# Two input channels become one work item over pairs of PSUM banks in the filter stage of a convolution kernel, and two small outputs change their PSUM pool

## The chip, the cores and the metric

The kernel runs on one core of a Trainium2 chip. The metric is the device time of one execution in microseconds (us). The profile and the trace come from one execution taken by the hardware profiler. Engines: PE is the matrix engine (PEld its weight loads), DVE the vector engine, ACT the scalar engine, POOL the GpSimd engine, SP the queue that issues most of the DMAs. PSUM has eight banks of 2 KB a partition, each of which holds 128x512 fp32 values[...].

## The reference

Two layers on an input of (4, 512, 512, 16). The change concerns the filter of the first layer only:

```python
# layer 0: x = x + conv(groupnorm(x)), with a filter given as a ratio of polynomials
a = jnp.pad(denumerator, ((0, 0), (0, 0), (1, 0), (1, 0)), constant_values=1.0)
b = jnp.pad(numerators, ((0, 0), (0, 0), (0, 0), (1, 0), (1, 0)), constant_values=0.0)
H_truncated = jnp.fft.rfft2(b, s=(l1, l2)) / jnp.fft.rfft2(a, s=(l1, l2))   # 512 x 512, 16 x 16 channels
h_truncated = jnp.fft.irfft2(H_truncated, s=(l1, l2))
H = jnp.fft.rfft2(h_truncated, s=(2 * l1, 2 * l2))
H_full = h0 + H[0]
X = jnp.fft.rfft2(x, s=(2 * l1, 2 * l2), axes=(-3, -2))
y = jnp.fft.irfft2(jnp.einsum('...hwi,ijhw->...hwj', X, H_full), ...)[..., :l1, :l2, :]
# layer 1: x = x + a 3x3 convolution of groupnorm(x) with norms, arccos and tanh
```

Numerator and denominator are polynomials of 9 x 9 terms for each of 16 x 16 pairs of channels (i in, j out).

## The kernel before

The kernel is a chain of stages. `filter_phase`, the first, computes the filter and writes it to `g_d` in DRAM; the transform of the input, the product with the filter, the way back and the second layer follow and are not touched. During the filter stage a generator, `beside`, also computes statistics of the input: one BATCH_NORM_STATS2 on DVE in every second step of the loop.

**Items.** A work item is (j, kp, h, i): output channel j, half kp of the frequencies k1 (two chunks k of 128, on the partitions), half h of the frequencies k2 (128, on the free axis), input channel i. There are 16 x 2 x 2 x 16 = 1024 items, and the loop takes two neighbouring i at a time, so 512 pairs, 32 for each j. One pass of the loop is called a step, p.

**A pair passes through three steps** (`new`, `mid`, `last`), so that a step works on three pairs:

- new: `polynomials` (L349): for each of the two channels two PSUM tiles of one bank each, pa (denominator) and pb (numerator), shape [128, k, c, 128] with c real or imaginary; sixteen recorded matmuls. `evict` on ACT: copy of pa to SBUF as `a` (L357), the squares of its real part to `sq` (L359) and of its imaginary part in place (L360).
- mid: `products` on DVE: m = pb·a (L366), x = pb·a with c swapped (L368), dn = the two squares added (L370). `terms` on POOL (L374, L375): numerator times conjugate denominator. Later in the step DVE's reciprocal of dn (L504), and `quotient` on POOL, sp = m/|a|² (L379).
- last: `edge` on ACT for h = 0: column k2 = 0 of sp is replaced from z (L384). `taps` (L395): 32 recorded matmuls of sp with a constant, into two PSUM tiles `pg`. `placed` on ACT: four copies of pg into the stage `st` (L406), which goes to `g_d` when i has run through.

**Beside it runs `odd(j - 1)`**: it reads back g_d of the output channel before (`ev_in`, L433), multiplies by a constant (`pt`, L447), copies (`ot`, L452) and writes to g_d (L453). `next(rest)` stands twice in a step, and each time copies the pt before and issues the next (four recorded matmuls of 128x512). For the first j there is nothing of it yet. After the loop the last `odd` runs alone.

**Rare parts.** `quad` runs in steps with p % 16 = 0, 2, 4 and 14: eight small matmuls into the PSUM tile `pu` (L332) and an ACT copy to `u` (L335), the polynomials over k1 of four channels, used two steps later. `weights(j + 1)` spreads over some ten steps of each j; once in it, four matmuls go into the tile `pz` (L285), and ACT copies it to `zs` (L293).

**PSUM.** Three pools share the eight banks: `ps_ab` with four buffers (pa and pb of two channels), `ps_g` with two (`pg`), `ps_t` with two, tag `t`, shared by pt, pu and pz:

```python
pt = ps_t.tile([P, 32 * C], F32, name="pt", tag="t")
pu = ps_t.tile([P, 2, N // 2], F32, name="pu", tag="t")
```

**Order.** `InOrder` keeps PE, DVE, ACT and POOL in the order in which the program issues. SP is ordered by a scheduler. In a step the order on PE is: pt (first `next(rest)`), the taps of `last`, the polynomials of `new`, pt (second `next(rest)`), and then pu or pz if it is their turn. On ACT: copy of the pt before, `edge`, `placed`, copy of the pt before, `evict`, then u or zs.

Of the kernel before, what the change touches and what calls it, by code (L numbers as in the profile page):

```python
# [40 lines left out]
F32 = mybir.dt.float32  # L41
# [3 lines left out]
PSUM = bass.MemoryType.PSUM  # L45

P = 128
N = 512
B = 4
C = 16  # L50
# [151 lines left out]
def bc(ap, axis, shape):  # L202
    return ap.unsqueeze(axis).to_broadcast(shape)
# [24 lines left out]
def filter_phase(tc, cst, h0, num, den, g_d, beside):  # L228
    nc = tc.nc
    with ExitStack() as ctx:  # L230
# [3 lines left out]
        ew = ctx.enter_context(tc.tile_pool(name="f_ew", bufs=2))  # L234
        stp = ctx.enter_context(tc.tile_pool(name="f_stage", bufs=4))
        evp = ctx.enter_context(tc.tile_pool(name="f_even", bufs=2))
        odp = ctx.enter_context(tc.tile_pool(name="f_odd", bufs=2))
        ps_ab = ctx.enter_context(tc.tile_pool(name="f_psab", bufs=4, space=PSUM))
        ps_g = ctx.enter_context(tc.tile_pool(name="f_psg", bufs=2, space=PSUM))
        ps_t = ctx.enter_context(tc.tile_pool(name="f_pst", bufs=2, space=PSUM))  # L240

        e1 = load_const(nc, cp, cst, "e1")
        e2 = load_const(nc, cp, cst, "e2").rearrange("p (s h n) -> p s h n", s=2, h=2)
# [5 lines left out]
        polys = {}  # L249

        def weights(j):
# [19 lines left out]
            v = sm.tile([18, 2, 4, C], F32, name="v")  # L271
            ev = sm.tile([18, 2, 2, C], F32, name="ev")
            od = sm.tile([18, 2, 2, C], F32, name="od")
            for n, t in enumerate((sa, sb)):
                for c in range(2):
                    q = 9 * c
# [3 lines left out]
            nc.vector.tensor_add(v[:, :, 0::2, :], ev, od)  # L280
            nc.vector.tensor_sub(v[:, :, 1::2, :], ev, od)
            yield
            pz = ps_t.tile([P, 4, 2, 4, C], F32, name="pz", tag="t")
            for k in range(4):
                nc.tensor.matmul(  # L285
                    pz[:, k].rearrange("p c v i -> p (c v i)"),
# [2 lines left out]
                    start=True,  # L289
                    stop=True,  # L290
# [29 lines left out]
            z = wt.tile([P, 4, 2, C], F32, name="z")  # L320
# [4 lines left out]

        def quad(j, kp, iq):

            pu = ps_t.tile([P, 2, N // 2], F32, name="pu", tag="t")
            for n in range(2):
                for i in range(4):  # L330
                    at = 32 * (i ^ 2 * n)
                    nc.tensor.matmul(pu[at : at + 32, n], polys[j][n][:, 4 * iq + i],  # L332
                                     e1[:, kp * (N // 2) : (kp + 1) * (N // 2)], start=True, stop=True)
            u = wt.tile([P, 2, N // 2], F32, name="u", bufs=6)
            nc.scalar.copy(u, pu)  # L335
            us[j, kp, iq] = u

        def polynomials(pair):

            for w in pair:
                w["pp"] = [ps_ab.tile([P, 2, 2, P], F32, name=f"pab{n}", tag="ab") for n in range(2)]
            for k in range(2):
                for w in pair:
                    for n in range(2):
                        at = 32 * (w["i"] % 4 ^ 2 * n)
                        q = slice(at, at + 18)
                        nc.tensor.matmul(  # L349
                            w["pp"][n][:, k].rearrange("p c n -> p (c n)"),  # L350
                            w["u"][q, n, k * P : k * P + P], e2[q, n, w["h"], :], start=True, stop=True,
                        )

        def evict(w):
            pa, _ = w["pp"]
            w["a"] = ew.tile([P, 2, 2, P], F32, name="a", bufs=4)
            nc.scalar.copy(w["a"], pa)  # L357
            w["sq"] = ew.tile([P, 2, P], F32, name="sq", bufs=4)
            nc.scalar.activation(w["sq"], pa[:, :, 0], AF.Square)  # L359
            nc.scalar.activation(pa[:, :, 1], pa[:, :, 1], AF.Square)  # L360

        def products(w):

            (pa, pb), a = w.pop("pp"), w["a"]
            w["m"] = ew.tile([P, 2, 2, P], F32, name="m", bufs=4)
            nc.vector.tensor_mul(w["m"], pb, a)  # L366
            w["x"] = ew.tile([P, 2, 2, P], F32, name="x", bufs=2)
            nc.vector.tensor_mul(w["x"], pb, a[:, :, ::-1])  # L368
            w["dn"] = ew.tile([P, 2, P], F32, name="dn", bufs=3)
            nc.vector.tensor_add(w["dn"], w["sq"], pa[:, :, 1])  # L370

        def terms(w):
            m, x = w["m"], w["x"]
            nc.gpsimd.tensor_add(m[:, :, 0], m[:, :, 0], m[:, :, 1])  # L374
            nc.gpsimd.tensor_sub(m[:, :, 1], x[:, :, 1], x[:, :, 0])  # L375

        def quotient(w):
            w["sp"] = ew.tile([P, 2, 2, P], F32, name="sp", bufs=4)
            nc.gpsimd.tensor_mul(w["sp"], w["m"], bc(w["dn"], 2, [P, 2, 2, P]))  # L379

        def edge(w):
            if w["h"] == 0:
                kp = w["kp"]
                nc.scalar.copy(w["sp"][:, :, :, 0], w["z"][:, 2 * kp : 2 * kp + 2, :, w["i"]])  # L384

        def taps(pair):

            kp, i, h, j = (pair[0][k] for k in ("kp", "i", "h", "j"))
            pg = [ps_g.tile([P, 2, 2, 4, 32], F32, name=f"pg{u}", tag="pg") for u in range(2)]
            for n, w in enumerate(pair):  # L390
                for k in range(2):
                    for c in range(2):
                        for u in range(2):
                            q = slice(64 * u, 64 * u + 64)
                            nc.tensor.matmul(  # L395
                                pg[u][:, n, k].rearrange("p a x -> p (a x)"), w["sp"][q, k, c, :],
                                dinv[q, 2 * kp + k, c, :], start=(c == 0), stop=(c == 1),
                            )
            return pg

        def placed(pair, st, pg):

            kp, i, h, j = (pair[0][k] for k in ("kp", "i", "h", "j"))
            for u in range(2):
                for a in range(2):
                    nc.scalar.copy(  # L406
                        st[a].rearrange("p (q k u x) i -> p u k q x i", q=2, k=2, u=2)[:, u, :, :, :, i : i + 2],
                        pg[u][:, :, :, 2 * a : 2 * a + 2].rearrange("p n k q x -> p k q x n"),
                    )
            if i == C - 2:  # L410
                for a in range(2):
                    for q in range(2):
                        nc.sync.dma_start(
                            out=dram(g_d[h], None, a * G_ROW // 2 + ((32 * q + 16 * kp) * C + j) * 8 * C,
                                     [C * 8 * C, 16], [1, 8 * C]),
                            in_=st[a].rearrange("p (q r e) i -> p q r (e i)", q=2, e=8)[:, q],
                        )
# [41 lines left out]
        def odds():  # L459

            for j in range(C):
# [2 lines left out]
                yield from odd(j)  # L464

        work = [dict(j=j, h=h, i=i, kp=kp)
                for j in range(C) for kp in range(2) for h in range(2) for i in range(C)]
        done, us = [0], {}
        order = InOrder(tc, nc.tensor, nc.vector, nc.scalar, nc.gpsimd)
        rest = odds()  # L470
# [1 line left out]
            pass  # L472
        quad(0, 0, 0)
        coming = iter(())
        n_pairs = len(work) // 2
        for p in range(n_pairs + 2):
            new, mid, last = (work[2 * (p - k) : 2 * (p - k) + 2] if 0 <= p - k < n_pairs else [] for k in range(3))
            with order:
                next(rest)
            if last:  # L480
                if last[0]["i"] == 0:
                    st = [stp.tile([P, N // 2, C], F32, name=f"st{a}", tag="st") for a in range(2)]
                with order:
                    for w in last:
                        edge(w)
                    placed(last, st, taps(last))
                done[0] += 2
                for w in last:
                    w.clear()
            with order:  # L490
                for w in mid:
                    products(w)
                    terms(w)
            if new:
                for w in new:
                    w["u"], w["z"] = us[w["j"], w["kp"], w["i"] // 4], polys[w["j"]][2]
                with order:
                    polynomials(new)
            with order:
                next(rest)  # L500
                for w in new:
                    evict(w)
                for w in mid:
                    nc.vector.reciprocal(w["dn"], w["dn"])  # L504
                    quotient(w)
                j, kp, r = p // 32, p // 16 % 2, p % 16
                if r in (0, 2, 4) and p < n_pairs:
                    quad(j, kp, r // 2 + 1)
                elif r == 14 and p + 2 < n_pairs:
                    quad(j + kp, 1 - kp, 0)  # L510
                if p % 32 == 4 and j + 1 < C:
                    coming = weights(j + 1)
                next(coming, None)
                if p % 2:
                    next(beside, None)
# [914 lines left out]
```

## Time and profile before

| | |
|---|---|
| median of 3 runs | 16929.8 us (16927.85 to 16944.9) |
| the profiled execution | 16971.28 us, its span 16969.5 us |
| filter loop in the trace, first polynomial matmul to last taps | 23 to 3760 us |
| mean granted PE clock | 0.969; 1.00 from 600 to 3400 us |
| busy in the stretch 600 to 1000 us (400 us) | PE 387.96, DVE 367.14, POOL 301.47, ACT 261.40, PEld 225.64 us |
| DMA share and rate there | 0.83, 241 GB/s |

The program's stages have different limits, so that the shares of the whole span say little about the filter stage; a window inside of it says more. A matmul that the page calls busy is a pipelined one: its record is longer than the time after which the next can follow. Times from one start to the next are therefore used below where an engine's pace matters.

From the second j on the steps repeat. Measured from the first taps matmul of a step to that of the next, the 32 steps of j = 3, at 736.23 to 969.62 us, take 8.67 us eight times (the steps with a quad; one of them 8.87), 8.72 us once (the step with pz), 6.79 us ten times and 6.69 us thirteen times. The ten are steps at whose start `edge` stands (h = 0), the thirteen such without it.

### The profile page before, as it was taken

The page shows a single profiled execution, that of the slowest core. Times are in us where ns is not written, and L with a number is a line of the kernel's source. Part 1 is how long each engine was busy: PE and PEld are TensorE (multiplying, and loading weights), DVE is VectorE, ACT ScalarE, POOL GpSimd, SP SyncE. Part 2 cuts the span into 40 slices and gives each one's busy share as a digit, 9 for nine tenths or more (in the row PEclk, how much of TensorE's full clock was granted, in tenths as well). Part 3 has the DMA queues.
Part 4 walks back from the last instruction along what each step waited for, and adds up shares of the span by engine and source line. Part 5 has one row for each costly group of instructions (what it writes and reads, how often), then busy time and mean ns, then how long its engine had stood idle before and what let it go on. Part 6 is the DMA issues. An engine that isn't in the chain of part 4 may idle for free. (4 is left out here: it accounts for less than half of the span.)

```text
span 16969.5 us, 546571 instructions
## 1 busy us (share of the span) xinstructions
PE 15334.3 (90%) x233100; PEld 11354.6 (67%) x233100; DVE 10569.6 (62%) x22267; ACT 9051.1 (53%) x18799; POOL 10185.7 (60%) x10637
## 2 busy tenths in 40 slices
PE   7999999999998888889888888888888888988888
PEld 5555555554447777777777777777777777877777
DVE  8999999973335555555555555555555553347877
ACT  5666666652225555555555555555555552017888
POOL 7777777761116666666666666666666661137766
PEclk7999999999999999999999999999999999989999
DMA  4888888887658888888888888888888886885531
GB/s 135 235 236 238 232 233 242 232 237 222 187 179 320 321 323 324 320 322 320 317 325 324 323 323 323 320 318 323 320 325 323 320 311 246 295 293 174 166 112 69
DMA packets 2914701, 4543.45 MB, mean 268 GB/s; under 512 B 126114, under 2 KB 2094460, under 8 KB 2801422
## 3 DMA queue, kind: packets, MB, share of 16 engines
q1 hardware_dynamic: 2703070, 3836.37, 66.5%
q0 software_dynamic: 172336, 605.00, 9.3%
q10 hardware_dynamic: 36864, 67.13, 1.1%
q8 instruction: 1837, 30.10, 0.7%
q14 instruction: 594, 4.87, 0.1%
HBM read 3030.71 MB, written 1477.31 MB: 266 GB/s over the span
## 5 line engine op out<-in xcount | busy, mean ns | idle before, releaser
L822 PE MATMUL pg<-c_dg,g 64*128 64x128 f32 x32832 | 2834.4, 291 | 329.7 <-ACT gh L722 163.9
L838 PE MATMUL pm<-xe,gh 128*32 128x64 f32 x131328 | 2405.5, 222 | 571.9 <-issue 342.4
L838 PEld LDWEIGHTS pm<-xe,gh 128*32 128x32 f32 x131328 | 2015.6, 110 | 1175.5 <-issue 1001.6
L822 PEld LDWEIGHTS pg<-c_dg,g 64*128 64x128 f32 x32832 | 2281.4, 190 | 667.6 <-issue 264.5
L867 DVE TENSOR_TENSOR z<-zq,pz 128x256 f32<-128x256 f32 x2052 | 861.5, 420 | 2628.3 <-ACT zq L866 2547.9
L720 DVE COPY gh<-pg 128x512 f32<-128x512 f32 x2046 | 1410.2, 689 | 1295.3 <-PE pg L822 1292.4
L447 PE MATMUL pt<-ev_in,c_todd 128*128 128x512 f32 x4096 | 1925.3, 609 | 108.8 <-ACT u L335 83.4
L791 POOL TENSOR_TENSOR xu<-xe,c_late 128x256 f32<-128x256 f32 x2052 | 1391.1, 701 | 859.3 <-ACT xe L722 834.4
L504 DVE RECIPROCAL dn<-dn 128x256 f32<-128x256 f32 x1024 | 1718.3, 1719 | 0.0
L722 ACT COPY yf<-pm 128x512 f32<-128x512 f32 x2046 | 1209.8, 591 | 931.0 <-PE pm L838 916.8
L379 POOL TENSOR_TENSOR sp<-m,dn 128x512 f32<-128x512 f32 x1024 | 1301.0, 1272 | 615.1 <-DVE dn L504 527.5
L802 ACT COPY xe<-xl 64x1024 f32<-64x1024 f32 x513 | 538.4, 1049 | 1875.2 <-POOL xl L793 1875.2
L722 ACT COPY gh<-pg 128x512 f32<-128x512 f32 x2058 | 1200.1, 584 | 401.0 <-PE pg L822 393.3
L447 PEld LDWEIGHTS pt<-ev_in,c_todd 128*128 128x128 f32 x4096 | 727.7, 189 | 1020.1 <-issue 701.0
L859 PE MATMUL pz<-c_ident,yf 128*128 128x128 f32 x8208 | 1375.7, 291 | 36.6 <-issue 23.6
L395 PEld LDWEIGHTS pg<-c_dinv,sp 64*128 64x128 f32 x16384 | 1009.1, 196 | 465.6 <-ACT sp L384 212.5
L406 ACT COPY st<-pg 128x256 f32<-128x256 f32 x2048 | 617.0, 392 | 1284.2 <-PE pg L395 1284.2
L793 POOL TENSOR_TENSOR xl<-xl,xu 128x1024 f32<-128x1024 f32 x513 | 1209.2, 2357 | 40.2
L395 PE MATMUL pg<-c_dinv,sp 64*128 64x128 f32 x16384 | 1110.8, 288 | 71.8 <-ACT sp L384 49.2
L875 POOL TENSOR_TENSOR zd<-z 128x512 f32<-128x512 f32 x513 | 652.4, 1272 | 795.4 <-DVE z L867 795.3
L1273 PE MATMUL pc<-l_band,xn 128*128 128x160 f32 (+2 forms) x6144 | 1074.9, 333 | 53.0 <-DVE e_o L1328 52.9
L907 POOL DMA_DIRECT2D y_d<-yo x511 | 296.5, 580 | 1347.0 <-ACT yo L722 1321.1
(201 smaller groups left out, 31021.0 us busy)
## 6 DMA issues: line engine op xcount, KB each, us to landing
xe<-xf_d SPq DMA_DIRECT2D x1026, 1536.0 KB
g<-g_d SPq DMA_DIRECT2D x511, 1024.0 KB
g_d<-st SPq DMA_DIRECT2D x256, 1024.0 KB
ev_in<-g_d SPq DMA_DIRECT2D x1024, 256.0 KB
g_d<-ot SPq DMA_DIRECT2D x1024, 256.0 KB
xf_d<-xe POOLq DMA_DIRECT2D x513, 448.0 KB, 8.3
xf_d<-xl POOLq DMA_DIRECT2D x513, 448.0 KB, 5.2
x_d<-xo SPq DMA_DIRECT2D x128, 1024.0 KB
```

The costliest lines, as they stand in the source:

```text
L379: nc.gpsimd.tensor_mul(w["sp"], w["m"], bc(w["dn"], 2, [P, 2, 2, P]))
L395: nc.tensor.matmul(pg[u][:, n, k].rearrange("p a x -> p (a x)"), w["sp"][q, k, c, :], dinv[q, 2 * kp + k, c, :], start=(c == 0), stop=(c = ...
L447: nc.tensor.matmul(pt, todd[:, c, kc, hh * P : hh * P + P], ev[:, kc, c], start=(kc == 0), stop=(kc == 1),)
L504: nc.vector.reciprocal(w["dn"], w["dn"])
L720: nc.vector.tensor_copy(dst, src)
L722: nc.scalar.copy(dst, src)
L791: nc.gpsimd.tensor_mul(u[:, :, h, c], xe[:, :, h, 1 - c], bc(late[:, 1 + c], 2, [P, F, 2]))
L793: nc.gpsimd.tensor_add(xl.rearrange("p f h c k -> p (f h c k)"), xl.rearrange("p f h c k -> p (f h c k)"), u.rearrange("p f h c k -> p (f ...
L822: nc.tensor.matmul(pg[c][:, j % 4], g[half, j], dg[half], start=True, stop=True)
L838: nc.tensor.matmul(pm[32 * q : 32 * q + 32, g % 8], gh[:, f].rearrange("p c j -> p (c j)"), xe[:, :, f].rearrange("p t h c k -> p t (h c k ...
L859: nc.tensor.transpose(pz[:, t % 4].rearrange("p v q x -> p (v q x)"), y[:, at].rearrange("p g x -> p (g x)"), ident)
L1273: nc.tensor.matmul(pc[:, lo:hi, :].rearrange("p w j -> p (w j)"), xns[q][:, h * P + dh : h * P + dh + P], bands[dh][:, o : o + hi - lo, :] ...
```

## The change

A pair of channels becomes one item. Its pa, pb, a, m, x and sp get a further axis v for the two channels: [128, v, k, c, 128], which in PSUM are two neighbouring banks, one for each v. `ps_ab` has two buffers of two banks in place of four of one. Matmuls still write one bank each, in the same order; the copy, the two squares, the three DVE operations, the two POOL operations of `terms` and the edge copy each cover both channels in one instruction. The reciprocal and the product of `quotient` stay separate for each v.

`pu` and `pz` are taken from `ps_g` (tag `pg`) and no longer from `ps_t`, which now serves pt alone. Of the SBUF buffers, `sq` now holds one pair (before: two), `x` one pair (as before), `dn` two pairs (before: one and a half); `a`, `m` and `sp` hold two pairs as before.

The instruction lists of PE are the same before and after. DVE has 1536 rows less, ACT 1536 and POOL 1024. On SP the same DMAs are issued; their order differs only by a place or a few around the loads of the weights and one write of `ot` in each j.

```diff
-        ps_ab = ctx.enter_context(tc.tile_pool(name="f_psab", bufs=4, space=PSUM))
+        ps_ab = ctx.enter_context(tc.tile_pool(name="f_psab", bufs=2, space=PSUM))
...
-            pz = ps_t.tile([P, 4, 2, 4, C], F32, name="pz", tag="t")
+            pz = ps_g.tile([P, 4, 2, 4, C], F32, name="pz", tag="pg")
...
-            pu = ps_t.tile([P, 2, N // 2], F32, name="pu", tag="t")
+            pu = ps_g.tile([P, 2, N // 2], F32, name="pu", tag="pg")
...
+        sh = [P, 2, 2, 2, P]
+
+        def polynomials(w):
+
+            i, kp = w["i"], w["kp"]
+            u = us[w["j"], kp, i // 4]
+            w["pp"] = [ps_ab.tile(sh, F32, name=f"pab{n}", tag="ab") for n in range(2)]
             for k in range(2):
-                for w in pair:
+                for v in range(2):
                     for n in range(2):
-                        at = 32 * (w["i"] % 4 ^ 2 * n)
+                        at = 32 * ((i + v) % 4 ^ 2 * n)
                         q = slice(at, at + 18)
                         nc.tensor.matmul(
-                            w["pp"][n][:, k].rearrange("p c n -> p (c n)"),
-                            w["u"][q, n, k * P : k * P + P], e2[q, n, w["h"], :], start=True, stop=True,
+                            w["pp"][n][:, v, k].rearrange("p c n -> p (c n)"),
+                            u[q, n, k * P : k * P + P], e2[q, n, w["h"], :], start=True, stop=True,
                         )
+        def flat(t):
+            return t.rearrange("p v k c n -> p (v k) c n")
+
         def evict(w):
-            pa, _ = w["pp"]
-            w["a"] = ew.tile([P, 2, 2, P], F32, name="a", bufs=4)
-            nc.scalar.copy(w["a"], pa)
-            w["sq"] = ew.tile([P, 2, P], F32, name="sq", bufs=4)
+            pa = flat(w["pp"][0])
+            w["a"] = ew.tile(sh, F32, name="a")
+            nc.scalar.copy(flat(w["a"]), pa)
+            w["sq"] = ew.tile([P, 4, P], F32, name="sq", bufs=1)
             nc.scalar.activation(w["sq"], pa[:, :, 0], AF.Square)
             nc.scalar.activation(pa[:, :, 1], pa[:, :, 1], AF.Square)
...
-            w["m"] = ew.tile([P, 2, 2, P], F32, name="m", bufs=4)
-            nc.vector.tensor_mul(w["m"], pb, a)
-            w["x"] = ew.tile([P, 2, 2, P], F32, name="x", bufs=2)
-            nc.vector.tensor_mul(w["x"], pb, a[:, :, ::-1])
-            w["dn"] = ew.tile([P, 2, P], F32, name="dn", bufs=3)
+            w["m"] = ew.tile(sh, F32, name="m")
+            nc.vector.tensor_mul(flat(w["m"]), pb, a)
+            w["x"] = ew.tile(sh, F32, name="x", bufs=1)
+            nc.vector.tensor_mul(flat(w["x"]), pb, a[:, :, ::-1])
+            w["dn"] = ew.tile([P, 4, P], F32, name="dn")
             nc.vector.tensor_add(w["dn"], w["sq"], pa[:, :, 1])
...
         def quotient(w):
-            w["sp"] = ew.tile([P, 2, 2, P], F32, name="sp", bufs=4)
-            nc.gpsimd.tensor_mul(w["sp"], w["m"], bc(w["dn"], 2, [P, 2, 2, P]))
+            w["sp"] = ew.tile(sh, F32, name="sp")
+            for v in range(2):
+                dn = w["dn"][:, 2 * v : 2 * v + 2]
+                nc.vector.reciprocal(dn, dn)
+                nc.gpsimd.tensor_mul(w["sp"][:, v], w["m"][:, v], bc(dn, 2, [P, 2, 2, P]))
 
         def edge(w):
             if w["h"] == 0:
-                kp = w["kp"]
-                nc.scalar.copy(w["sp"][:, :, :, 0], w["z"][:, 2 * kp : 2 * kp + 2, :, w["i"]])
+                kp, i = w["kp"], w["i"]
+                nc.scalar.copy(w["sp"][:, :, :, :, 0],
+                               polys[w["j"]][2][:, 2 * kp : 2 * kp + 2, :, i : i + 2].rearrange("p k c v -> p v k c"))
...
```

The rest of the diff rewrites `taps`, `placed` and the loop for one item in place of a list of two, with the operations in the order they had.

More of the change, by code (lines that the diff above doesn't have):

```diff
@@ L336, in quad @@
             us[j, kp, iq] = u
-        def polynomials(pair):
-            for w in pair:
-                w["pp"] = [ps_ab.tile([P, 2, 2, P], F32, name=f"pab{n}", tag="ab") for n in range(2)]
+        sh = [P, 2, 2, 2, P]
[3 more added lines that the diff above has]
+            w["pp"] = [ps_ab.tile(sh, F32, name=f"pab{n}", tag="ab") for n in range(2)]
             for k in range(2):
-                for w in pair:
+                for v in range(2):
                     for n in range(2):
-                        at = 32 * (w["i"] % 4 ^ 2 * n)
+                        at = 32 * ((i + v) % 4 ^ 2 * n)
                         q = slice(at, at + 18)
                         nc.tensor.matmul(
-                            w["pp"][n][:, k].rearrange("p c n -> p (c n)"),
-                            w["u"][q, n, k * P : k * P + P], e2[q, n, w["h"], :], start=True, stop=True,
-                        )
+                            w["pp"][n][:, v, k].rearrange("p c n -> p (c n)"),
+                            u[q, n, k * P : k * P + P], e2[q, n, w["h"], :], start=True, stop=True,
+                        )
+        def flat(t):
+            return t.rearrange("p v k c n -> p (v k) c n")
         def evict(w):
-            pa, _ = w["pp"]
-            w["a"] = ew.tile([P, 2, 2, P], F32, name="a", bufs=4)
-            nc.scalar.copy(w["a"], pa)
-            w["sq"] = ew.tile([P, 2, P], F32, name="sq", bufs=4)
+            pa = flat(w["pp"][0])
+            w["a"] = ew.tile(sh, F32, name="a")
+            nc.scalar.copy(flat(w["a"]), pa)
+            w["sq"] = ew.tile([P, 4, P], F32, name="sq", bufs=1)
             nc.scalar.activation(w["sq"], pa[:, :, 0], AF.Square)
@@ L362, in products @@
         def products(w):
-            (pa, pb), a = w.pop("pp"), w["a"]
-            w["m"] = ew.tile([P, 2, 2, P], F32, name="m", bufs=4)
-            nc.vector.tensor_mul(w["m"], pb, a)
-            w["x"] = ew.tile([P, 2, 2, P], F32, name="x", bufs=2)
-            nc.vector.tensor_mul(w["x"], pb, a[:, :, ::-1])
-            w["dn"] = ew.tile([P, 2, P], F32, name="dn", bufs=3)
+            (pa, pb), a = (flat(t) for t in w.pop("pp")), flat(w["a"])
+            w["m"] = ew.tile(sh, F32, name="m")
[3 more added lines that the diff above has]
+            w["dn"] = ew.tile([P, 4, P], F32, name="dn")
             nc.vector.tensor_add(w["dn"], w["sq"], pa[:, :, 1])
         def terms(w):
-            m, x = w["m"], w["x"]
+            m, x = flat(w["m"]), flat(w["x"])
             nc.gpsimd.tensor_add(m[:, :, 0], m[:, :, 0], m[:, :, 1])
@@ L377, in quotient, with taps @@
         def quotient(w):
-            w["sp"] = ew.tile([P, 2, 2, P], F32, name="sp", bufs=4)
-            nc.gpsimd.tensor_mul(w["sp"], w["m"], bc(w["dn"], 2, [P, 2, 2, P]))
+            w["sp"] = ew.tile(sh, F32, name="sp")
[3 more added lines that the diff above has]
+                nc.gpsimd.tensor_mul(w["sp"][:, v], w["m"][:, v], bc(dn, 2, [P, 2, 2, P]))
         def edge(w):
             if w["h"] == 0:
-                kp = w["kp"]
-                nc.scalar.copy(w["sp"][:, :, :, 0], w["z"][:, 2 * kp : 2 * kp + 2, :, w["i"]])
-        def taps(pair):
-            kp, i, h, j = (pair[0][k] for k in ("kp", "i", "h", "j"))
+                kp, i = w["kp"], w["i"]
+                nc.scalar.copy(w["sp"][:, :, :, :, 0],
+                               polys[w["j"]][2][:, 2 * kp : 2 * kp + 2, :, i : i + 2].rearrange("p k c v -> p v k c"))
+        def taps(w):
+            kp = w["kp"]
             pg = [ps_g.tile([P, 2, 2, 4, 32], F32, name=f"pg{u}", tag="pg") for u in range(2)]
-            for n, w in enumerate(pair):
+            for n in range(2):
                 for k in range(2):
@@ L395, in taps @@
                             nc.tensor.matmul(
-                                pg[u][:, n, k].rearrange("p a x -> p (a x)"), w["sp"][q, k, c, :],
+                                pg[u][:, n, k].rearrange("p a x -> p (a x)"), w["sp"][q, n, k, c, :],
                                 dinv[q, 2 * kp + k, c, :], start=(c == 0), stop=(c == 1),
@@ L399, in taps, with placed @@
             return pg
-        def placed(pair, st, pg):
-            kp, i, h, j = (pair[0][k] for k in ("kp", "i", "h", "j"))
+        def placed(w, st, pg):
+            kp, i, h, j = (w[k] for k in ("kp", "i", "h", "j"))
             for u in range(2):
@@ L466, in filter_phase @@
         work = [dict(j=j, h=h, i=i, kp=kp)
-                for j in range(C) for kp in range(2) for h in range(2) for i in range(C)]
+                for j in range(C) for kp in range(2) for h in range(2) for i in range(0, C, 2)]
         done, us = [0], {}
@@ L474, in filter_phase @@
         coming = iter(())
-        n_pairs = len(work) // 2
-        for p in range(n_pairs + 2):
-            new, mid, last = (work[2 * (p - k) : 2 * (p - k) + 2] if 0 <= p - k < n_pairs else [] for k in range(3))
+        for p in range(len(work) + 2):
+            new, mid, last = (work[p - k] if 0 <= p - k < len(work) else None for k in range(3))
             with order:
                 next(rest)
[L480 to L485, printed above, removed]
-                    placed(last, st, taps(last))
[L487 to L497, printed above, removed]
+                if last:
+                    if last["i"] == 0:
+                        st = [stp.tile([P, N // 2, C], F32, name=f"st{a}", tag="st") for a in range(2)]
+                    edge(last)
+                    placed(last, st, taps(last))
+                    done[0] += 2
+                    last.clear()
+                if mid:
+                    products(mid)
+                    terms(mid)
+                if new:
                     polynomials(new)
-            with order:
                 next(rest)
[L501 to L505, printed above, removed]
+                if new:
+                    evict(new)
+                if mid:
+                    quotient(mid)
                 j, kp, r = p // 32, p // 16 % 2, p % 16
-                if r in (0, 2, 4) and p < n_pairs:
+                if r in (0, 2, 4) and p < len(work):
                     quad(j, kp, r // 2 + 1)
-                elif r == 14 and p + 2 < n_pairs:
+                elif r == 14 and p + 2 < len(work):
                     quad(j + kp, 1 - kp, 0)
```

## The prediction

> **What bounds the kernel now.** The change lies in the filter loop alone, so I read in this order: the page's row of the loop's dearest PE operation with what ended its idle time, a window inside the loop, and the trace in order of time through single steps.
>
> The window from 600 to 1000 us (start and end, length, then busy us of PE, PEld, DVE, ACT and POOL, granted clock, DMA share, GB/s):
>
> ```profile
> 600.00:1000.00 400.00, 387.96 (x3306) 225.64 (x3304) 367.14 (x485) 261.40 (x734) 301.47 (x345) 1.00 0.83 241
> ```
>
> PE is busy for 97% and DVE for 92%. Either could be the bound. The steps decide it. One without `edge`, at 1027.62 us:
>
> ```profile
> 1027.62 2.06 PE L395 MATMUL pg<-c_dinv,sp 64*128 64x128 f32 x32
> 1029.60 1.15 PE L349 MATMUL pab<-c_e,u 18*128 18x256 f32 x16
> 1030.68 3.70 PE L447 MATMUL pt<-ev_in,c_todd 128*128 128x512 f32 x8
> 1034.31 2.06 PE L395 MATMUL pg<-c_dinv,sp 64*128 64x128 f32 x32
> ```
>
> Each group starts when the one before it has been fed: taps 1.98, polynomials 1.08, pt 3.63, together 6.69 us with no wait of PE in between. That is PE's own pace, and 13 of 32 steps have it. A step with `edge` is longer by 0.10 us:
>
> ```profile
> 1002.65 1.20 ACT L406 COPY st<-pg 128x256 f32<-128x256 f32 x4 [2.05 <-PE pg L395]
> ...
> 1007.09 0.30 ACT L384 COPY sp<-z 128x4 f32<-128x4 f32 x2
> ...
> 1007.35 1.86 PEld L395 LDWEIGHTS pg<-c_dinv,sp 64*128 64x128 f32 x32 [0.85 <-ACT sp L384]
> ```
>
> ACT waits 2.05 us for the taps, then works without a pause from 1002.65 to `edge`, and the next taps wait for `edge`: a loop of 2.09 + 4.70 = 6.79 us. A step with a quad, from taps at 736.23:
>
> ```profile
> 741.20 0.63 PE L332 MATMUL pu<-c_e,sa 18*32 18x256 f32 x8
> 741.66 0.61 PE L332 MATMUL pu<-c_e,sb 18*32 18x256 f32 x8
> 742.35 0.58 ACT L335 COPY u<-pu 128x512 f32<-128x512 f32 x1
> 742.99 1.98 PE L447 MATMUL pt<-ev_in,c_todd 128*128 128x512 f32 x4 [0.72 <-ACT u L335]
> 744.90 1.86 PEld L395 LDWEIGHTS pg<-c_dinv,sp 64*128 64x128 f32 x32 [0.76 <-issue]
> ```
>
> pu ends at 742.27. The next pt doesn't need u, but it gets pu's buffer of `ps_t`, and PE stands for 0.72 us until ACT has emptied it. Over the program that is, in the page's row of pt (busy, mean ns, idle before and its main releaser):
>
> ```profile
> L447 PE MATMUL pt<-ev_in,c_todd 128*128 128x512 f32 x4096 | 1925.3, 609 | 108.8 <-ACT u L335 83.4
> ```
>
> 83.4 us, and the list of groups adds 9.5 us for the same wait on zs (pz).
>
> **What the Trainium skill says.** Perfetto Trace Analysis, section Optimization Strategy: a gap that repeats on the engine that should be saturated can mean that PSUM lacks room for the next tile. The trace agrees: the same 0.72 us in each quad step. The same page, Optimizing Scalar/DVE Operations, puts the cost of an instruction's access to PSUM at about 125 ns on DVE and 51 ns on ACT and says that grouping helps "if the engine is saturated". Here DVE's start-to-start times, 0.60 us for 512 elements (L366 to L368) and 0.33 for 256 (L370), leave 0.06 us fixed; ACT's, 0.48 (L357) and 0.28 (L360), leave 0.08. I use the trace's. Advanced Engine Details and Errata, The Read-Write Bubble, says that one instruction may read several PSUM banks on trn2. No row of before does so.
>
> **Part by part.**
>
> 1. *pu and pz move to `ps_g`.* pt then only needs a pt buffer that ACT emptied in the first half of the step (L452 at 739.37), so it starts when pu has been fed, at 742.27. The wait of 83.4 + 9.5 = 92.9 us goes. What is late next? pu now needs a pg buffer: `placed`, which empties both, runs from 738.31 to 739.52, and pu comes at 741.20, 1.7 us of slack. The next taps need the buffer that u empties by 742.93; they would come at 742.27 + 1.91 = 744.18, 1.2 us of slack. They also need `edge`, on ACT behind u and one copy (0.48 each), at about 743.3 and done by 743.6, 0.6 us of slack. A quad step becomes 7.95 us, the pz step 8.04. Cost put at nothing, gain 93; if pg collided in every quad step, the gain would be between 0 and 93.
>
> 2. *ACT's merged operations.* From one more 256 elements = 0.20 us: copy 0.48 + 0.40 = 0.88, square to sq 0.46 + 0.20 = 0.66, square in place 0.48, together 2.02 us for 2.43 (1004.18 to 1006.61). ACT's loop falls to about 6.4 us, below PE's 6.69, so that the ten edge steps of a j give 0.10 each: 10 x 15 x 0.10 = 15 us. The rest is covered by PE's work. The merged `edge` saves ACT 0.09 but the first tap waited for the first of the two only; taken as nothing.
>
> 3. *DVE's merged operations.* Per step now 3.06 us (1004.86 to 1007.92) + two reciprocals of 1.66 and 1.61. New: 1.14 + 1.14 + 0.60 = 2.88 + 3.27 = 6.15 us; with a BATCH_NORM_STATS2 (0.60) in every second step and about 0.08 for `weights`, 6.53. Below 6.69, so worth nothing from the second j on: PE covers it. But m now waits for the whole copy: it starts 0.68 + 0.40 = 1.08 us after the copy's start, at 3.62 + 1.08 = 4.70 us after the taps' start, and dn ends at 4.70 + 2.88 = 7.58. The next polynomials, which overwrite these banks, come at 6.69 + 1.98 = 8.67: 1.1 us of slack, which a step with statistics or `weights` work shortens to about 0.4. Queued behind m on DVE are x, dn and the reciprocals; POOL's second product would end at about 7.58 + 3.3 + 1.3 = 12.2, and `edge` wants it at 13.1. That fits also, if not by much.
>
> 4. *POOL's merged operations*: two rather than four, 1.24 us each by L379, for 3.0 us in all before. POOL idles 25%; nothing. `sq` and `x` with one buffer: sq waits for a dn that ended at 7.58 - 6.69 = 0.9 us of the step, when ACT comes at 4.5; x for a POOL subtraction some 4 us before. Nothing. PE's list is unchanged, SP's reordered by a place or two around loads that have a whole j of time; SP itself idles. Nothing.
>
> 5. *The first j* (23 to about 270 us) has no pt, PE's clock stands at 0.59 to 0.74, and steps last 7.2 us on average. There the half with `edge` is set by ACT's loop through the slow taps (gain 0.41), the other nearer DVE (0.18): 16 x 0.41 + 16 x 0.18 = 9; I take 8, bounds 0 and 15.
>
> Sum: 93 + 15 + 8 = 116 us. Against the profiled execution's 16971.3 that gives 16855; the median of the runs shown stands 41 us (0.24%) below it, so 16929.8 - 116 = **16814 us**.
>
> Not shown before: an ACT or DVE operation over two banks. The nearest 1024-element row is ACT's L802 at 1049 ns for 591 of L722's 512, 0.23 us per 256: slightly dearer than assumed, still inside ACT's 0.3 us of slack. From below, a saving of more than the fixed part is excluded, and PE's pace allows no step under 6.69. For DVE I take linear growth; twice the fixed part would be 6.7 us a step, just PE's pace.
>
> **Rivals.**
>
> - *DVE becomes the bound* (the slower side). Place: m, x and dn. The average step of before is 7.28 us (8 of 8.67, one of 8.72, 10 of 6.79, 13 of 6.69); with 3.27 + 0.38 beside them, the three operations must exceed 3.63 us, 1.26 times the 2.88 assumed, to lose. At 1.35 times, 7.54 us a step, 480 steps lose 0.26 each: 125 us, 17055. For it: DVE's 92%. Against: its time has been proportional to the elements wherever two sizes can be compared. Chance 0.07.
> - *The chain gets longer and eats part of the gain*: merged operations end later (point 3), and with statistics the slack of 0.4 to 1.1 us runs out; or pg comes late (point 1). At 0.15 us in 480 steps 72 us are lost: 16886. Chance 0.10.
> - *DMA takes over.* The loop moves the same bytes in 7.05 us a step, so its share rises from 0.83 to 0.86. For it: small packets (under 2 KB for nearly all). Against: PE's waits for ev_in are short. Half the gain lost: 16870. Chance 0.08.
> - *As worked out*, 16795 to 16840: chance 0.75.
>
> **How the numbers follow.** A change of 0.2% (34 us) is about what a measurement here can tell from none. Faster: 0.75 and most of the two middle cases, 0.88; within 0.2%: 0.05; slower: 0.07. The range 16780 to 16890 takes in the bounds of points 2 and 5 and the middle rivals, and leaves out the slower side.
>
> **What would show it.** After: the row of pt without a wait on ACT u; quad steps of 7.95 us and all others of 6.69; DVE's m and x near 1.22 us as recorded (0.68 + 0.54), dn near 0.68, ACT's copy near 1.0; taps without a wait on `edge`. It is wrong if polynomials wait for DVE, if taps or pu wait for u or `placed`, or if plain steps exceed 6.7 us.

## The result, and the profile after

The changed kernel takes 16815.85 us (median of 4 runs, 16806.05 to 16827.89); the kernel before, run beside it, 16933.77 us. The ratio is 0.993, with a 95% interval of 0.9913 to 0.9947: 118 us less. The prediction was 116 us less and 16814 us.

The profiled execution of after took 16827.89 us (span 16826.1), 143 us less than that of before. Of these, 120.8 us are gained by the start of the loop's last taps (3756.9 us before, 3636.1 after). The other 22.6 us lie in the stages behind, whose code is unchanged. A second trace of the same kernel, told of below, shows what they are worth.

The row of pt, from the page of after (busy, mean ns, idle before and its main releaser), and the same window inside the loop as before (length, then PE, PEld, DVE, ACT and POOL busy, granted clock, DMA share, GB/s):

```profile
L455 PE MATMUL pt<-ev_in,c_todd 128*128 128x512 f32 x4096 | 1927.4, 609 | 15.3 <-DMA ev_in<-g_d 15.2
```

```profile
600.00:1000.00 400.00, 400.00 (x3432) 235.12 (x3431) 376.62 (x342) 251.26 (x563) 296.73 (x244) 1.00 0.84 242
```

The wait on u is gone from the row; what is left was there before. PE is busy for all of the window, and DVE, with some 30% fewer instructions, is busier than before (376.62 us for 367.14), because more steps fit into the window. (Over the whole kernel ACT has 1792 instructions less, 18799 before and 17007 after, and not the 1536 named under The change: the merged `edge` adds 256.) The DMA share rose from 0.83 to 0.84, and PE waits for no transfer here.

A step with a quad, from the trace of after in order of time (start, us, engine, line, operation; in brackets the idle time before and its releaser; here and in the fences below, lines of other work in between are left out):

```profile
721.66 0.63 PE L332 MATMUL pu<-c_e,sa 18*32 18x256 f32 x8
722.12 0.61 PE L332 MATMUL pu<-c_e,sb 18*32 18x256 f32 x8
722.66 1.98 PE L455 MATMUL pt<-ev_in,c_todd 128*128 128x512 f32 x4
722.81 0.59 ACT L335 COPY u<-pu 128x512 f32<-128x512 f32 x1 [0.31 <-PE pu L332]
723.77 0.22 ACT L391 COPY sp<-z 128x8 f32<-128x8 f32 x1
724.57 0.52 PEld L403 LDWEIGHTS pg<-c_dinv,sp 64*128 64x128 f32 x8 [0.76 <-ACT sp L391]
```

pt follows pu at once, and ACT copies u while it runs. `edge` is done at 723.99, more than half a microsecond before PE is ready for the taps; the 0.76 us of PEld beside its name is the same time that PEld stands behind a running pt in steps without `edge` too, so the name is not the cause.

From j = 2 on a j looks like this: quad steps 7.88 us (8.67 before), one of them 8.22 (8.78 to 8.87), the step with pz 7.97 (8.72), and the 23 others 6.69. The sum for j = 3 is 225.30 us for 233.39. Recounted, 12 of the 32 steps of before took 6.79 us and 11 took 6.69, where the sections above say ten and thirteen.

### The profile page after: what moved, and what is told of

It is laid out like the page before. It is cut to its first block, busy times and chain, and to the rows that moved or that the text cites. A ratio compares the mean times of both kernels' runs of the same rounds, so it can differ in the third digit from the quotient of the medians.

```text
span 16826.1 us, 539027 instructions
## 1 busy us (share of the span) xinstructions
PE 15300.8 (91%) x233100; PEld 11353.7 (67%) x233100; DVE 10513.0 (62%) x20731; ACT 8877.3 (53%) x17007; POOL 10040.5 (60%) x9613
## 5 line engine op out<-in xcount | busy, mean ns | idle before, releaser
L894 PE MATMUL py<-z,c_ig 128*64 128x256 f32 x6156 | 1068.2, 408 | 39.7 <-issue 37.4
```

## The experiments

The times in the table are medians beside those of the kernel before on the same chip, and the ratio is the first by the second. "Loop" is the start of the last taps in the one trace of each kernel, "behind" the rest of the span.

| kernel | us, before beside it | ratio, 95% interval | loop | behind |
|---|---|---|---|---|
| before | | | 3756.9 | 13212.6 |
| after | 16815.9, 16933.8 | 0.993, 0.9913 to 0.9947 | 3636.1 | 13190.0 |
| e1_pools_only | 16833.4, 16938.8 | 0.9939, 0.9926 to 0.9952 | 3659.5 | 13153.3 |
| e2_pairs_only | 16915.6, 16938.8 | 0.9987, 0.9979 to 0.9995 | 3735.4 | 13177.3 |
| e3_after_again | 16818.3, 16938.8 | 0.9928, 0.9914 to 0.9941 | 3638.0 | 13174.5 |
| e4_evict_split | 16900.2, 16938.8 | 0.9977, 0.9969 to 0.9984 | 3717.9 | 13178.2 |
| e5_dve_split | 16843.5, 16958.4 | 0.9940, 0.9926 to 0.9953 | 3648.5 | 13219.8 |
| e6_dve_plus_256 | 16920.3, 16958.4 | 0.9980, 0.9972 to 0.9988 | 3736.5 | 13169.4 |
| e7_dve_plus_512 | 17008.2, 16958.4 | 1.0034, 1.0022 to 1.0046 | 3812.7 | 13181.9 |
| e8_recip_one_step_later | 16822.3, 16958.4 | 0.9925, 0.9913 to 0.9938 | 3631.3 | 13196.3 |
| e9_dn_before_x | 16817.3, 16938.4 | 0.9922, 0.9907 to 0.9936 | 3631.3 | 13193.4 |
| e10_plus_256_dn_before_x | 16877.0, 16938.4 | 0.9968, 0.9955 to 0.9980 | 3696.3 | 13177.0 |

The last column scatters over 66 us with no relation to the edit, although the code there is the same. The loop column is the sharper measure of a change in the loop, and it is used below wherever the times can't tell. Two traces of the same kernel, after and e3, differ by 1.9 us in it.

### The two halves of the change

e1 is the kernel before with this alone:

```diff
-            pz = ps_t.tile([P, 4, 2, 4, C], F32, name="pz", tag="t")
+            pz = ps_g.tile([P, 4, 2, 4, C], F32, name="pz", tag="pg")
...
-            pu = ps_t.tile([P, 2, N // 2], F32, name="pu", tag="t")
+            pu = ps_g.tile([P, 2, N // 2], F32, name="pu", tag="pg")
```

> The kernel before, with pu and pz alone moved to the pool of pg; all operations stay one per channel. Theory (the wait of pt on the ACT copy of u is the larger part, and the move alone removes it): quad steps 7.9 us for 8.67, the step with pz 8.0, the steps with edge stay at 6.79; about 6.9 us a j over 14.5 j, so 100 us, 16834 us. Rival (the move needs the shorter ACT work of the pairs, since otherwise the next taps wait for u or for edge behind it): quad steps between 8.2 and 8.67, 16870 to 16930 us.

e2 is the kernel after with the same two lines turned back.

> The kernel after, with pu and pz back in the pool of pt; the pairs stay. Theory: the wait of pt on u stays at 0.65 to 0.72 us, since u cannot start before pu ends; quad steps stay near 8.6, the steps with edge fall to 6.69 (15 us), the first j gives 7 us: about 25 us in all, 16908 us. Rival (the merged operations carry the gain): under 16870 us.

The rows of pt from the pages of e1 and of e2:

```profile
L447 PE MATMUL pt<-ev_in,c_todd 128*128 128x512 f32 x4096 | 1927.0, 609 | 16.1 <-DMA ev_in<-g_d 16.0
```

```profile
L455 PE MATMUL pt<-ev_in,c_todd 128*128 128x512 f32 x4096 | 1927.9, 609 | 108.5 <-ACT u L335 83.4
```

With the pools alone the wait is gone, with the pairs alone all 83.4 us of it are there. e1 gains 97.4 us in the loop (105 in the medians): quad steps 7.88 us, steps with `edge` still 6.79. e2 gains 21.4 us in the loop (23 in the medians): steps with `edge` 6.69, quad steps still 8.67, one 9.01. 97.4 + 21.4 = 118.8, and both together give 118.9 (e3) or 120.8 us (after): the halves add up and don't need each other. In e1, where ACT's operations are still one per channel, the next taps come as early as in after:

```profile
746.97 0.63 PE L332 MATMUL pu<-c_e,sa 18*32 18x256 f32 x8
747.97 1.98 PE L447 MATMUL pt<-ev_in,c_todd 128*128 128x512 f32 x4
748.12 0.59 ACT L335 COPY u<-pu 128x512 f32<-128x512 f32 x1
749.08 0.31 ACT L384 COPY sp<-z 128x4 f32<-128x4 f32 x2
749.88 1.86 PEld L395 LDWEIGHTS pg<-c_dinv,sp 64*128 64x128 f32 x32 [0.76 <-ACT sp L384]
```

The rival, that the move needs the shorter ACT work, is out: `edge` ends at 749.39, half a microsecond before the taps.

### The same kernel a second time

> The kernel after, unchanged, for a comparison on the same chip and for a second trace. The filter loop should end 121 us earlier than before again. The stages behind it are the same code, so that the further 22 us by which the first trace of after was ahead of before at its end should not come back as a fixed amount.

The loop ended 118.9 us earlier than before, 1.9 us from the first trace; j = 3 has 225.30 us in both. The stages behind took 13174.5 us for 13190.0. So the extra 22.6 us of the first pair of profiles are scatter.

### What the pairs are worth on ACT and on DVE

e4 undoes the pairs on ACT alone:

```diff
-            nc.scalar.copy(flat(w["a"]), pa)
...
-            nc.scalar.activation(w["sq"], pa[:, :, 0], AF.Square)
-            nc.scalar.activation(pa[:, :, 1], pa[:, :, 1], AF.Square)
+            for v in range(2):
+                r = slice(2 * v, 2 * v + 2)
+                nc.scalar.copy(w["a"][:, v], pa[:, r])
+                nc.scalar.activation(w["sq"][:, r], pa[:, r, 0], AF.Square)
+                nc.scalar.activation(pa[:, r, 1], pa[:, r, 1], AF.Square)
```

> The kernel after, with ACT's copy and two squares done for each channel of the pair (six instructions, each within one bank) in place of three over both banks; DVE and POOL stay merged, so that m waits for the second copy, about 0.8 us later than in after. Theory: ACT's loop through edge is back at 6.79 us in ten steps of a j (15 us), and the slack of dn against the next polynomials, 1.1 us in after, falls to 0.3 us and runs out in steps with statistics: 16816 plus 15 to 60 us. Rival (ACT and the chain have room to spare): 16816 plus 0 to 5 us.

It lost 82 us against e3 (80 in the loop), more than the theory's 60. By the length of the steps, the loss in the loop has three main parts:

- `edge` steps take 6.91 us, not 6.79. In 12 steps of each of 15 j, the 0.10 us up to 6.79 were expected, 18 us; the 0.12 us beyond it were not, 22 us.
- The step of 8.22 us takes 9.10, the one four steps before it 7.11 for 6.69, and another 6.77. That is 1.38 us a j, 21 us.
- The first j takes 245.9 us for 230.1, 16 us. What costs them there is open.

The 0.12 us come from the second channel's copy: it starts 0.40 us behind the square before it (751.09 and 751.49 us in the trace of e4), where in the kernel before it was 0.28. In the trace of e4 this copy waits for a semaphore that ACT's own operations raise; in that of before, where the two channels lie in separate tiles, it doesn't. The only one of ACT's operations that can still be open then is the square. So the copy probably waits for the end of the square, although it doesn't read what the square writes; no run takes this wait away.

That the chain runs out is seen in the step of 9.10, from the trace of e4:

```profile
833.42 1.21 DVE L374 TENSOR_TENSOR x<-pab,a 128x1024 f32<-128x1024 f32 x1
834.55 0.68 DVE L376 TENSOR_TENSOR dn<-sq,pab 128x512 f32<-128x512 f32 x1
834.78 1.64 PE L350 MATMUL pab<-c_e,u 18*128 18x256 f32 x16 [0.65 <-DVE x L374]
835.28 0.74 PEld L350 LDWEIGHTS pab<-c_e,u 18*128 18x128 f32 x14 [0.24 <-DVE dn L376]
```

PE stands before the polynomials, first for x and then for dn.

e5 undoes the pairs on DVE alone:

```diff
-            nc.vector.tensor_mul(flat(w["m"]), pb, a)
...
-            nc.vector.tensor_mul(flat(w["x"]), pb, a[:, :, ::-1])
...
-            nc.vector.tensor_add(w["dn"], w["sq"], pa[:, :, 1])
+            for v in range(2):
+                r = slice(2 * v, 2 * v + 2)
+                nc.vector.tensor_mul(flat(w["m"])[:, r], pb[:, r], a[:, r])
+                nc.vector.tensor_mul(flat(w["x"])[:, r], pb[:, r], a[:, r, ::-1])
+                nc.vector.tensor_add(w["dn"][:, r], w["sq"][:, r], pa[:, r, 1])
```

> The kernel after, with DVE's m, x and dn done for each channel of the pair (six instructions over one bank each); ACT and POOL stay merged. Theory: DVE needs 0.18 us more a step, which PE covers except in the one step of a j behind the z reciprocal (8.22 us in after, then about 8.4) and in the first j (about 3 us): 16816 plus 3 to 8 us. Rival (DVE sets the pace, so its merge earned the time): 0.18 us in 480 steps, plus 86 us.

The intervals of e5 and e3 overlap, so the times don't decide. In the loop it lost 10.5 us against e3: plain steps stay at 6.69, 8.22 becomes 8.57, and another step of each j 7.12, together 0.78 us a j. That is the theory's place at a little over its size, and far from the rival's 86 us. Start to start, the six operations took 3.06 us, as in before; the three merged ones with the reciprocal behind them take 1.14 + 1.13 + 0.71 = 2.98. The merge saved DVE 0.08 us a step and not the 0.18 expected.

### How near DVE is

e6 adds the line marked + to after, a repeat of half of dn; e7 adds a repeat of the whole dn in its place.

```diff
             nc.vector.tensor_add(w["dn"], w["sq"], pa[:, :, 1])
+            nc.vector.tensor_add(w["dn"][:, 0:2], w["sq"][:, 0:2], pa[:, 0:2, 1])
```

> The kernel after, with the first half of dn computed twice: 0.33 us more of DVE in each step, output unchanged. Theory: DVE at about 6.9 us a step, still under the mean step of 7.04, but over the plain step of 6.69, so that its lag grows by some 0.2 us a step until the slack before the polynomials (about 0.9 us) is used up: plus 10 to 40 us, in steps behind statistics and weights. Rival (DVE has room): no change. Rival (DVE is already the bound): 0.33 x 512, plus 165 us.

> The kernel after, with the whole dn computed twice: 0.60 us more of DVE in each step, output unchanged. Theory: DVE at about 7.15 us a step passes PE's mean of 7.04 and becomes the bound: plus 50 to 110 us. Rival (DVE has room): under plus 20 us. Rival (DVE is already the bound): 0.60 x 512, plus 300 us.

Both fell between the theory and the rival that DVE is already the bound: in the loop 100 and 177 us more than after, where 10 to 40 and 50 to 110 were expected. The larger part of the difference lies in DVE's step, as the trace of e6 has it:

```profile
914.10 1.21 DVE L372 TENSOR_TENSOR x<-pab,a 128x1024 f32<-128x1024 f32 x1
915.23 0.68 DVE L374 TENSOR_TENSOR dn<-sq,pab 128x512 f32<-128x512 f32 x1
915.94 0.42 DVE L375 TENSOR_TENSOR dn<-sq,pab 128x256 f32<-128x256 f32 x1
916.39 3.36 DVE L386 RECIPROCAL dn<-dn 128x256 f32<-128x256 f32 x2
919.67 0.63 DVE L580 BATCH_NORM_STATS2 stats<-xs 128x6 f32<-128x512 f32 x1
```

From dn to its repeat are 0.71 us and from there to the reciprocal 0.45, where 0.60 and 0.33 stand between independent operations of these sizes in before (0.60 behind m, 0.33 behind dn):

```profile
1006.06 0.41 DVE L370 TENSOR_TENSOR dn<-sq,pab 128x256 f32<-128x256 f32 x1
1006.39 0.68 DVE L366 TENSOR_TENSOR m<-pab,a 128x512 f32<-128x512 f32 x1
1006.99 0.68 DVE L368 TENSOR_TENSOR x<-pab,a 128x512 f32<-128x512 f32 x1
1007.59 0.41 DVE L370 TENSOR_TENSOR dn<-sq,pab 128x256 f32<-128x256 f32 x1
```

DVE's step in e6 is then 1.12 + 1.13 + 0.71 + 0.45 + 1.67 + 1.61 = 6.69 us, just PE's own pace. So every statistics operation (0.60) becomes lag, work by which DVE falls behind PE, and only quad steps pay it back. In e7 the step is 6.96, with statistics and `weights` work 7.34, over PE's mean of 7.04. In after itself it is 1.14 + 1.13 + 0.71 + 3.28 = 6.26 us, with 0.38 for the rest 6.64.

A smaller part of the loss is not DVE's but the clock's. Two passes of the same quad step of e6, from taps to taps (length, then PE, PEld, DVE, ACT and POOL busy, granted clock, DMA share, GB/s):

```profile
820.73:829.95 9.22, 8.61 (x73) 4.68 (x73) 9.15 (x9) 4.86 (x10) 7.20 (x9) 1.00 0.31 91
1746.98:1759.49 12.51, 11.90 (x74) 5.50 (x73) 12.37 (x12) 4.86 (x10) 9.96 (x11) 0.73 0.30 91
```

In both, PE waits 0.2 us for DVE's x and 0.4 for dn before the polynomials. In the second the clock is granted at a half for 6.8 us behind that wait, and the same matmuls take longer. From the third j on, e6 has 34 us of half clock in all and e7 27; e10 below has 3.4, and before, after and e1 to e5 have none. Measured by the same step in other j, it cost e6 some 15 of its 100 us, and e7 some 13 of 177. Why the drop follows this wait in some j and not in others, the runs don't show.

e10 is e6 with dn and its repeat ahead of x, so that the reciprocal no longer stands directly behind the dn that it reads.

> The kernel with the first half of dn computed twice, and both placed before x. Output unchanged. Theory (the addition cost 100 us in the loop because DVE's step, with the 0.11 us behind dn and again behind the repeat, came to 6.69 us, PE's own pace, so that every statistics operation became lag): without those waits DVE needs about 6.5 us, and the loss falls from 100 us to between 20 and 60 us against after. Rival (the loss comes from the length of the chain m, x, dn alone, which is as long as before): it stays at 90 to 110 us.

The loss fell to 60 us in the loop (3696.3 us), at the upper end of what was expected: the repeat still waits for dn (0.71 us), the reciprocal no longer, and DVE's step is 6.59 us. The rival, that the length of the chain alone counts, is out: some 13 of the 40 us between e6 and e10 are the clock's, but without them e6 still lost about 85 us and e10 about 58.

### The one slow quad step, and the best version

In each j one quad step of after takes 8.22 us. It follows the reciprocal of z that `weights` does once a j (from the trace of after):

```profile
798.58 0.95 DVE L312 RECIPROCAL z_den<-z_den 128x128 f32<-128x128 f32 x1
799.45 0.64 DVE L579 BATCH_NORM_STATS2 stats<-xs 128x6 f32<-128x512 f32 x1
800.00 1.20 DVE L370 TENSOR_TENSOR m<-pab,a 128x1024 f32<-128x1024 f32 x1
802.25 0.68 DVE L374 TENSOR_TENSOR dn<-sq,pab 128x512 f32<-128x512 f32 x1
802.64 1.13 PE L350 MATMUL pab<-c_e,u 18*128 18x256 f32 x10
```

dn ends at 802.93, after the polynomials of the next pair have come to need its banks. e8 lets the reciprocal come a step later, ahead of the room that a quad step leaves:

```diff
             yield
+            yield
             nc.vector.tensor_add(zd, dr, di)
             nc.vector.reciprocal(zd, zd)
```

> The kernel after, with one more step between the squares of z and its reciprocal, so that the 0.9 us reciprocal falls into a step with a quad. Theory (the step of 8.22 us is one in which the polynomials wait for a dn made late by that reciprocal): this step falls to about 7.9 and no other rises, 0.33 us in 14 j, 5 us, which the times can hardly tell from none; the trace shows it. Rival (the 8.22 us come from u or from pg): the step stays at 8.22.

The step is 7.88 us in every j from the second on, no other rose, and j = 3 takes 224.96 us for 225.30. The loop ends at 3631.3 us, 4.8 before after's. The medians can't show that (16822.3 us). e9 puts dn before x as well:

> The kernel with the z reciprocal one step later, and on DVE dn placed before x, so that the first reciprocal no longer stands directly behind the dn that it reads. Theory (in after the reciprocal starts 0.71 us behind dn, where the next independent operation started 0.60 behind: a wait of 0.11 for dn's result): DVE needs about 0.1 us less a step, the slack before the polynomials grows from 0.95 to about 1.05 us, and since PE sets the pace the time stays at 16818 within 10 us; only the first j can gain up to 3 us. Rival (DVE paces part of the loop still): plain steps fall under 6.69 or the loop gains more than 10 us.

```profile
877.46 1.23 DVE L370 TENSOR_TENSOR m<-pab,a 128x1024 f32<-128x1024 f32 x1 [0.24 <-ACT a L361]
```

```profile
876.96 1.22 DVE L371 TENSOR_TENSOR m<-pab,a 128x1024 f32<-128x1024 f32 x1 [0.47 <-ACT a L362]
878.10 0.68 DVE L373 TENSOR_TENSOR dn<-sq,pab 128x512 f32<-128x512 f32 x1
878.70 1.22 DVE L375 TENSOR_TENSOR x<-pab,a 128x1024 f32<-128x1024 f32 x1
879.83 1.74 DVE L386 RECIPROCAL dn<-dn 128x256 f32<-128x256 f32 x1
```

The first fence is after, the second e9, the same kind of step. dn takes 0.60 us to the next start and x 1.13, and DVE idles 0.47 us before m in place of 0.24. The loop ends where e8's does: PE paces it, and DVE's room is worth nothing until something fills it. e9's loop is the earliest together with e8's, and its median (16817.3 us) can't be told from after's. The slack before the polynomials stayed at 0.94 us, where 1.05 was expected: x, now last, ends as late as dn did, since m starts later.

## Why the prediction was right, point by point

**The wait of pt (point 1).** 93 us were predicted, e1 shows 97.4 in the loop. A quad step fell by 0.79 us rather than 0.72, because pt can start 1.00 us after pu does (721.66 to 722.66). The prediction had 1.07, since it took pu's recorded end for the moment at which pt can follow, though a matmul's record is longer than that, as is said under Time and profile before. Nothing took the wait's place: pu, u and `edge` all had the slack that was worked out, with or without the pairs.

**ACT's loop (point 2).** 15 us from ten steps a j; the mechanism and the 0.10 us were right, the number of steps was twelve, so 18 us. ACT's three operations take 0.90 + 0.70 + 0.49 = 2.09 us start to start where 2.02 were estimated (from the trace of after):

```profile
994.84 1.07 ACT L361 COPY a<-pab 128x1024 f32<-128x1024 f32 x1
995.74 0.67 ACT L363 ACTIVATE sq<-pab 128x512 f32<-128x512 f32 x1
996.44 0.58 ACT L364 ACTIVATE pab<-pab 128x512 f32<-128x512 f32 x1
996.93 0.59 ACT L460 COPY ot<-pt 128x512 f32<-128x512 f32 x1
```

The fixed part of ACT's copy, from 0.48 us for one bank and 0.90 for two, is 0.06 us. The prediction's 0.08 came from two unlike operations, a copy and a square.

**DVE (point 3).** It was taken as covered, and in plain steps it is. But the estimate of 6.53 us a step with everything was too low: 6.64, for want of the 0.11 us that the reciprocal waits behind dn. The slack of dn before the polynomials was given as 1.1 us, and as 0.4 in busy steps; in after it is 0.95 in plain steps, 0.12 in one step beside `weights`, and runs out once in a j, where 0.34 us are lost (8.22 for 7.88). That is the second rival's mechanism, at 5 us.

The first rival, DVE as the bound, did not come, but it was nearer than the factor of 1.26 on three operations said, which was measured against before's mean step: 0.45 us more of DVE in each step, a factor of 1.15, cost 100 us (e6). The mean was the wrong measure. In e10, DVE needs 6.59 + 0.38 = 6.97 us a step, less than PE's mean of 7.04, and the loop still lost 60 us. The plain steps of 6.69 us come in rows of up to nine, and a lag that grows in such a row is not paid back inside it.

**POOL and the buffers (point 4).** They were put at nothing. No run undoes them alone, so this is not shown.

**The first j (point 5).** 8 us predicted; 7.1 in after's trace, 4.9 in e3's, from the first taps of this j to those of the next. The number fits, the working doesn't show. It gave 0.41 us in each of 16 steps to ACT's loop, 6.6 us in all. But PE's waits for `edge` there fell only from 39.6 to 36.5 us in after and 37.7 in e3, and the waits of the polynomials for DVE's x, which the prediction named as a sign of being wrong, rose from 0.4 to 4.8 and 5.8 us. The clock granted over the first 262 us was 0.71 in before and 0.73 and 0.74 in the two traces of after. e2, which differs from after by the pools alone, was 3 to 5 us faster still there. Where the gain of the first j comes from stays open, and the agreement is luck.

**The sum.** 116 us predicted, 120.8 and 118.9 in the loops of the two traces, 118 and 120 in the medians. The mechanism of the two large terms is shown, but that the sum is off by only 2 to 5 us is partly luck: points 1 and 2 gave 4 and 3 us more than worked out, the slow quad step of each j cost 5 that nothing was set down for, and the first j gave 1 to 3 us less. The third rival, DMA, is not seen: the share rose by 0.01, and PE's idle time before pt is the 15 us of before.

## What to carry to other kernels

Read what each rare tile shares its PSUM buffers with: a matmul that needed nothing from ACT waited for a copy because a tile used in a quarter of the steps rotated through its two buffers, and moving that tile to a pool which is empty at that moment was worth four fifths of the gain with no operation made cheaper. Merging operations on engines that are not the bound is worth only what they delay on the one that is; here 0.10 us in the steps where ACT closed a loop with PE. And the room of a second engine is to be counted over the longest row of short steps, with the waits between neighbours that depend on each other, not against the mean step.

## What the runs showed of the hardware that was not expected

- A DVE operation directly behind the one that it reads or overwrites started 0.11 to 0.12 us later than an independent one: 0.71 for 0.60 us behind a 128x512 addition, 0.45 for 0.33 behind a 128x256 one. In the fence of e6 that is 0.03 us after the recorded end of the one before it (915.91 and 915.94 us), where independent operations start before this end. With one other operation in between (e9) the 0.11 us were gone. ACT's second copy in e4 came late by the same 0.12 us, also 0.03 us after the recorded end of the square.
- An operation over two PSUM banks cost no more per element than one over a single bank: DVE's 128x1024 product 1.14 us start to start for twice 0.60, ACT's copy 0.90 for twice 0.48. The Trainium skill's statement that one instruction may read several PSUM banks (Advanced Engine Details and Errata, The Read-Write Bubble), which no row of before could show, holds here.
- Waits of PE of 0.2 to 1.2 us, in a step where DVE was late, were in some j followed by 3.4 to 10.2 us at half the clock (e6, e7), at a cost of 1.6 to 5 us each time.
